# Where rotations, scale splits, signs and the last attention blocks stand in the order of a fused attention and feed-forward kernel

## The chip, the cores and the metric

The kernel runs on one core of one Trainium2 chip. The metric is device time in microseconds (us) of one execution. A core has TensorE (PE in the profile), VectorE (DVE), ScalarE (ACT), GpSimd (POOL) and SyncE (SP), which here issues most of the DMAs. [...] A number such as L590 is a line of the kernel before.

## The reference, cut to what matters

All data is float32. B = 4 sequences of S = 512 tokens, E = 1024, 16 heads of 64; the feed-forward part has 8 experts.

```python
xn = layernorm(x)
# attention, for each sequence on its own
q, k, v = (xn @ Wq), (xn @ Wk), (xn @ Wv)           # (S, 16, 64)
q, k = rotary(q), rotary(k)                          # x * cos + swap(x) * sin
logits = where(causal, q @ k.T, -1e9) / 8
s = (softmax(logits) @ v).reshape(S, E) @ Wo
# gated feed-forward with weights of -1, 0, 1
routing = softmax(xn @ gate_w.T)                     # (tokens, 8)
in_scale, out_scale = routing @ in_channel_scale, routing @ out_channel_scale
f = ((xn * in_scale) @ sign(weight).T) * out_scale + bias
out = x + s * silu(f)
```

## The kernel before

**Order of work.** PE's instructions run in the order in which the program writes them. The orders of DVE, ACT, POOL and SP are decided by a scheduler when the kernel is built, from the dependences and the program order, except for the first sequence's layernorm at the start, where DVE and ACT follow the program too, and where the program pins single instructions (`keep_in_program_order`, among them the splits of scales, L682 to L685, one half of each sign, L697, and the sums of Wo, L981). So a step that the program moves takes with it what it issues on PE exactly, and on the other engines only about.

**Projections.** `projections(b)` is a generator that yields after each matmul. For each sequence it goes through ten keys (b, g, m): g is one of four groups of four heads, m is 0 for queries, 1 for keys and 2 for values (which serve two groups at once), in the order Q, K of group 0, V of groups 0 and 1, Q, K of group 1, and the same for groups 2 and 3. Each is computed as a seven-product (Strassen-Winograd) multiplication. `project_qk` (L329) issues 28 matmuls of 128x256; DVE forms the sums of weights (`form_w`, L295) and of inputs (`form_x`, L314), and joins products into the results c[0] and c[1] (L355, L390), one per unit i of the group. `project_v` issues 56.

**Rotation.** A result c becomes a rotated query or key in `rotary` (L316): ACT swaps its 32-row blocks into sw with four copies of 32x512 (L322, L323), DVE multiplies c by the cosines (L324), POOL multiplies sw by the sines (L325) and adds both (L326). Results that are not rotated yet stand in the list `turn`. Before the change, `project_qk` rotates its first result at its own end, for queries and keys alike, and the second one in whatever projection comes next, after that one's second product.

**Slots.** The attention phase has 16 slots k = (b, g). Slot k runs the attention of group k − 1 as a list of pieces, interleaved with 84 projection matmuls (`interleave`, L859; slot 0 has 76 and no attention): after each of n pieces some 84/n matmuls follow. The usual pieces are: five transposes of the probabilities of unit w (`transpose_p`, L568); `scores_1` of the present group, with `values(w)` of the one before; five transposes of unit v; `scores_3` with `values(v)`; a wait; `scores_02`; two waits. The score pieces put matmuls on PE (L508), then DVE adds the mask (L519) and takes the maximum (L523), ACT takes exponentials (L526), DVE a reciprocal (L534), and POOL normalizes (L536). `transpose_p` puts four transposes on PE (L574) and the copy of the PSUM bank to pT on ACT for banks 0, 2 and 4 (L580) and on DVE for 1 and 3 (L578). pT has one buffer, which all units share; the PSUM ring has four banks and the scores two double banks. `values` runs 16 matmuls (L590), DVE copies the result over v (L599), and SP stores it to at_d in DRAM (L600).

**What else lies in the slots.** In slot 0 the pieces are the three steps of the router (`router`, L608) and, between them, the loading and splitting of the two channel scales:

```python
pieces = [
    routing[0],
    lambda: (load_scales(in_scale), load_scales(out_scale)),
    routing[1],
    lambda: split_scales(isc),
    routing[2],
    lambda: split_scales(osc),
```

Router step 1 is a chain of small DVE operations that ends with rex (L627 to L650); step 2 transposes rex on PE (rt, L654) and stores it. `split_scales` (L672) is three DVE operations on 128x1024 (L682, L683, L685). Scales, staged weights for the signs and the next sequence's x tiles all go through one pool of two buffers, "x". `make_sign(n)` (L690) turns a staged weight tile into -1, 0, 1 with four DVE operations of 128x512 (L697, L698, twice each). Two signs are made in each of slots 4, 8, 12 and 13, by three inserted pieces: load at the slot's start, then one sign after four pieces, another after eight. In slots with g = 1 the first two x tiles of the next sequence are loaded at the slot's start; in slots with g of 2 and 3 they are normalized and transposed.

**The seam.** After slot 15 the projections are over (L936 on): the last result is rotated, the pools of the projections are closed, and bias, the eight halves of Wo (L959) and the first stored attention rows (`load_at`, L1022) are loaded. What is left of the attention is then interleaved with the feed-forward matmuls of the first pair of row tiles (`gated(0)`, L990), in steps of four matmuls: `dense(gates, n)` runs n steps and, where n is over 1, takes one of eight subtractions on DVE that form sums of Wo after each (`sum_wo`, L981). `split` makes a high part of the scaled input on ACT (hi, L755) and a low part on DVE (lo, L756); `out_scales` puts four matmuls on PE (os, L765) into the two score banks. The order there is:

```python
for n in range(5):
    transpose_p(w, n)
split(0, 0)
values(w)
```

then two steps of `dense`, v's transposes in pairs with two steps after each, `scores_1`, `values(v)`, two steps, `scores_3`, four steps, `out_scales`, the rest of `gated(0)`, and `scores_02`. After the seam come `gated(1)` and `project_out(q)` for eight pairs of row tiles, which the change does not touch.

Of the kernel before, what the change touches and what calls it, by code (L numbers as in the profile page):

```python
# [15 lines left out]
DVE = mybir.EngineType.DVE  # L16
# [35 lines left out]
def attn_gated_ffn_kernel(  # L52
# [15 lines left out]
    nc = tc.nc  # L68
# [33 lines left out]
    osc = cp.tile([P, E], F32R, name="osc")  # L102
# [62 lines left out]
    def load_x(b, t):  # L165
        if b == 0:
            xt = X1[:, t, :]
        else:
            xt = xip.tile([P, E], F32, tag="x", name=f"x_{b}_{t}")
        nc.sync.dma_start(out=xt, in_=x[(b * TPB + t) * P : (b * TPB + t + 1) * P, :])  # L170
        xin[b, t] = xt
# [141 lines left out]
        }[n]()  # L313
        nc.vector.tensor_tensor(f, x0, x1, op=ALU.subtract)  # L314

    def rotary(u, m, c):  # L316

        sc = SCALE if m == 0 else 1.0
        rot = qk.tile([P, S], F32, tag=f"rot{m}", name="rot%d_%d_%d_%d" % (m, *u))
        sw = tmp.tile([P, S], F32, tag="sw", name="sw%d_%d_%d_%d" % (m, *u))  # L320
        for r in range(0, P, 64):
            nc.scalar.activation(sw[r : r + 32, :], c[r + 32 : r + 64, :], AF.Copy, scale=sc)  # L322
            nc.scalar.activation(sw[r + 32 : r + 64, :], c[r : r + 32, :], AF.Copy, scale=sc)  # L323
        nc.vector.scalar_tensor_tensor(rot, c, sc, cos_sb, op0=ALU.mult, op1=ALU.mult)  # L324
        nc.gpsimd.tensor_tensor(sw, sw, sin_sb, op=ALU.mult)  # L325
        nc.gpsimd.tensor_tensor(rot, rot, sw, op=ALU.add)  # L326
        (Q, K)[m][u] = rot

    def project_qk(key):  # L329

        b, g, m = key
        pos = keys.index(key)
        after = keys[pos + 1] if pos + 1 < len(keys) else None
        a11, a12, a21, a22 = quarters_w(key)
        b11, b12, b21, b22 = quarters_x(b)
        un = "%d_%d_%d" % key
        c = [tmp.tile([P, S], F32, tag="c", name=f"c_{un}_{i}") for i in range(2)]

        def product(ps, wq, xq):
            for k in range(4):  # L340
                nc.tensor.matmul(  # L341
                    ps, lhsT=wq[:, k, :], rhs=xq[:, k, :], start=(k == 0), stop=(k == 3)
                )
                yield

        def halves(n):

            ps = bank(f"pj_{un}_{n}")
            return ps, ps[:, :TH], ps[:, TH:]

        def part(n):
            return tmp.tile([P, TH], F32, tag=f"part{n}", name=f"part_{un}_{n}", bufs=1)

        def add(out, ps, x):
            nc.vector.tensor_tensor(out, ps, x, op=ALU.add)  # L355

        _, p, r = halves(1)
        yield from product(p, a11, b11)
        yield from product(r, a12, b21)
        p1 = tmp.tile([P, S], F32, tag="part1", name=f"part_{un}_1", bufs=1)[:, :TH]  # L360
        nc.scalar.copy(p1, p)
        add(c[0][:, :TH], r, p1)
        if turn:
            rotary(*turn.pop(0))
        _, p, r = halves(2)
        yield from product(r, SF[key, 3], TF[b, 3])
        if pos == 0:

            bank3 = halves(3)
            yield from product(bank3[2], SF[key, 1], TF[b, 1])  # L370
        yield from product(p, SF[key, 2], TF[b, 2])
        u2, u3 = part(2), part(3)
        add(u2, p, p1)
        add(u3, r, u2)
        if after:
            form_w(after, 3)
        if pos:
            ps, p, r = halves(3)
            yield from product(r, SF[key, 1], TF[b, 1])
        else:  # L380
            ps, p, r = bank3
        if after:
            form_w(after, 1)
            if after[2] < 2:
                form_w(after, 2)
        yield from product(p, a22, TF[b, 4])
        p5 = tmp.tile([P, S], F32, tag="part1", name=f"part_{un}_5", bufs=1)[:, :TH]
        nc.scalar.copy(p5, r)
        nc.gpsimd.tensor_tensor(u2, u2, p5, op=ALU.add)
        nc.vector.tensor_tensor(  # L390
            c[1].rearrange("p (h n) -> p h n", h=2),
            ps.rearrange("p (h n) -> p h n", h=2),
            u3[:, None, :].to_broadcast((P, 2, TH)),
            op=ALU.add,
        )
        load_w()
        _, p, _ = halves(4)
        yield from product(p, SF[key, 4], b22)
        add(c[0][:, TH:], p, u2)
        if after and after[2] < 2:  # L400
            form_w(after, 4)

        turn.extend([((b, g, i), m, c[i]) for i in range(2)])
        rotary(*turn.pop(0))

    def project_v(key):

        b, g, _ = key
# [53 lines left out]
        if turn:  # L462
            rotary(*turn.pop(0))
        yield from product(7, SF[key, 3], TF[b, 3])
        yield from product(6, SF[key, 2], TF[b, 2])
        add(u2, 6, lambda n: by_group(p1, n))
        add(u3, 7, lambda n: quarter(n, *u2))
# [24 lines left out]
    turn = []  # L492
# [375 lines left out]
    for k, (b, g) in enumerate(groups):  # L868
        pieces = []
        if k > 0:  # L870
            pieces, late = attention_pieces(k - 1, late)
        extra = []
        if g == 0:
            routing = [lambda n=n: router(b, n) for n in range(3)]
            if k == 0:
                nothing = lambda: None
                pieces = [
                    routing[0],
                    lambda: (load_scales(in_scale), load_scales(out_scale)),
                    routing[1],  # L880
                    lambda: split_scales(isc),
                    routing[2],
                    lambda: split_scales(osc),
                    nothing,
                    nothing,
                    nothing,
                ]
            else:

                if b < B - 1:  # L890
                    pieces.insert(7, routing[0])
                pieces.insert(10, routing[1])
                pieces.insert(13, routing[2])
        elif g == 1 and b + 1 < B:
            for t in range(2):
                load_x(b + 1, t)
        elif g > 1 and b + 1 < B:
            t0 = 2 * (g - 2)
            for t in range(t0, t0 + 2):
                layernorm(b + 1, t)  # L900
            extra = [
                lambda t=t, h=h: transpose_x(b + 1, t, h) for t in range(t0, t0 + 2) for h in range(2)
            ]
            if g == 2:
                extra.append(lambda: [load_x(b + 1, t) for t in (2, 3)])

        step = max(1, (len(pieces) + len(extra)) // (len(extra) + 1))
        for n, e in enumerate(extra):
            pieces.insert(min(len(pieces), (n + 1) * step + n), e)
        if len(pieces) > 18:  # L910

            pieces.append(lambda: None)
        if k in (4, 8, 12, 13):
            n = {4: 0, 8: 2, 12: 4, 13: 6}[k]
            pieces.insert(8, lambda: make_sign(n + 1))
            pieces.insert(4, lambda: make_sign(n))
            pieces.insert(0, lambda: (load_sign(n), load_sign(n + 1)))
        if b == B - 1:

            if g < 2:  # L920
                load_xn(g)
            if g in (1, 2):
                pieces.insert(3, lambda: in_scales(g - 1, score_banks))
            if g == 3:
                z_place[0] = [xip.tile([P, E], F32, tag="x", name=f"z0_{i}") for i in range(2)]
                pieces.insert(3, lambda: out_scales(0, score_banks))
        if k == 11:

            pieces.append(lambda: router(b + 1, 0))
        interleave(pieces, fill, 3 * 7 * 4 if k else 3 * 7 * 4 - 8)  # L930
        if g == NGRP - 1:
            for _ in fill:
                pass
            if b + 1 < B:
                for n in (3, 1, 2, 4):
                    form_x(b + 1, n)  # L936
                fill = projections(b + 1)
    rotary(*turn.pop(0))
    pctx.close()


# [84 lines left out]


    u0, u1 = units = [(*groups[-1], i) for i in range(2)]
    w, v = late
    sums = iter([(n, c) for n in (1, 3) for c in range(4)])  # L1030

    def dense(gates, n):
# [4 lines left out]
                if nxt:  # L1037
                    sum_wo(*nxt)

    for n in range(5):  # L1040
        transpose_p(w, n)
    split(0, 0)
    values(w)
    gates = gated(0)
    dense(gates, 2)
    split(0, 1)
    for ns in ((0, 1), (2, 3), (4,)):
        for n in ns:
            transpose_p(v, n)
        if n < 4:  # L1050
            dense(gates, 2)
    scores_1(units)
    values(v)
    dense(gates, 2)
    scores_3(units)
    dense(gates, 4)

    split(1, 0)
    out_scales(1, score_banks)
    dense(gates, 4)  # L1060
    for _ in gates:
        pass
    split(1, 1)
# [211 lines left out]
```

## Time and profile before

| what | us |
|---|---|
| three runs | 1203.40, 1203.84, 1203.88 |
| median | 1203.84 |
| profiled execution, device time | 1206.14 |
| its span | 1204.4 |
| PE busy / DVE busy / ACT busy / POOL busy | 1177.4 / 768.6 / 494.8 / 550.6 |
| mean granted clock of PE | 0.992 |

The span is the time from the first to the last instruction in the trace; the device time has 1.74 us around it. PE's busy time counts overlapping matmuls once. PEclk in the page and in the windows is the clock that PE was granted, 1.00 being full speed; [...]. A wait "PE pv L590 <- ACT pT L580" says that PE stood ahead of its instruction of line 590 on tile pv until ACT had finished the one of line 580 on tile pT. A timeline row gives the start, the duration, the engine, the line, the operation and its tiles, and in brackets the idle time ahead of it with what ended it.

### The profile page before, as it was taken

To read this page: it belongs to the slowest core of one execution; us is meant where nothing else is said; L and a number is where in the kernel's file an instruction comes from. 1 tells how busy PE (TensorE), PEld (TensorE's weight loads), DVE (VectorE), ACT (ScalarE), POOL (GpSimd) and SP (SyncE) were. 2 spreads that over 40 slices of the span, in tenths; PEclk is the share of its full clock that TensorE was granted. 3 is DMA by queue.
4 is the path that set the end of the run, shared out by engine and by line. 5 is a ranking of instruction groups with operands and counts; after the bars stand their busy time and mean duration, and the time that the engine had idled before them with its cause. 6 is when DMAs were issued, how large, how long until landed. Compare 5 with 4: busy or idle time off the path is not lost.

```text
span 1204.4 us, 16112 instructions
## 1 busy us (share of the span) xinstructions
PE 1177.4 (98%) x5864; PEld 863.1 (72%) x5864; DVE 768.6 (64%) x1380; ACT 494.8 (41%) x1121; POOL 550.6 (46%) x597
## 2 busy tenths in 40 slices
PE   9899999999999999999999999999899999999998
PEld 8788777777777777877778787777565466545664
DVE  6767767875876687487759777755656633553353
ACT  2435734543664454275545426534543121222120
POOL 0535624541653455165435615443355455544544
PEclk9899999999999999999999999999899999999999
DMA  8321423313141341314145122210503523422320
GB/s 304 110 76 68 155 79 118 111 47 114 44 158 55 107 145 48 96 62 140 53 123 202 64 84 75 79 49 19 205 10 122 181 85 127 144 83 92 110 70 35
DMA packets 60016, 121.92 MB, mean 101 GB/s; under 512 B 5025, under 2 KB 40609, under 8 KB 53921
## 3 DMA queue, kind: packets, MB, share of 16 engines
q1 hardware_dynamic: 55072, 112.11, 28.3%
q0 software_dynamic: 4576, 8.39, 2.0%
q8 instruction: 46, 0.75, 0.3%
q10 hardware_dynamic: 288, 0.39, 0.1%
q14 instruction: 34, 0.27, 0.1%
HBM read 95.45 MB, written 25.43 MB: 100 GB/s over the span
## 4 chain that ended last, share of the span: by engine, by line
PE 78%; DVE 12%; ACT 7%; issue 2%; POOL 1%; DMA 0%; ACTq 0%; DVEq 0%; POOLq 0%
PE pj L341 22%; PE wo L1112 16%; PE pj L425 13%; PE ff L990 10%; PE pv L590 5%; PE sc L508 5%; PE ptp L574 5%; DVE nmx L523 2%; ACT sw L322 2%; ACT sw L323 2%; ACT p L526 2%; DVE S L295 1%; DVE sc L519 1%; PE xtp L210 1%; PE idle L782 1%
## 5 line engine op out<-in xcount | busy, mean ns | idle before, releaser
L536 POOL TENSOR_SCALAR p<-p,rs 128x128 f32<-128x128 f32 (+3 forms) x256 | 167.0, 665 | 245.5 <-DVE rs L534 243.4
L526 ACT ACTIVATE p<-sc,nmx 128x128 f32<-128x128 f32 (+3 forms) x256 | 132.6, 524 | 175.3 <-DVE nmx L523 167.7
L341 PE MATMUL pj<-X,w 128*128 128x256 f32 x576 | 138.8, 382 | 0.2 <-ACT X L216 0.2
L325 POOL TENSOR_TENSOR sw<-sw,sin_sb 128x512 f32<-128x512 f32 x64 | 86.5, 1352 | 91.5 <-ACT sw L323 83.9
L341 PE MATMUL pj<-T,S 128*128 128x256 f32 x512 | 123.5, 383 | 0.0
L341 PEld LDWEIGHTS pj<-X,w 128*128 128x128 f32 x576 | 105.2, 190 | 14.6 <-issue 1.8
L580 ACT COPY pT<-ptp 128x512 f32<-128x512 f32 x96 | 56.0, 586 | 140.7 <-PE ptp L574 136.1
L341 PE MATMUL pj<-T,w 128*128 128x256 f32 x448 | 109.0, 385 | 0.0
L523 DVE TENSOR_REDUCE nmx<-sc 128x2 f32<-128x512 f32 (+3 forms) x128 | 103.5, 819 | 2.5
L990 PE MATMUL ff<-sg,hi 128*128 128x512 f32 x256 | 104.5, 408 | 0.0
L574 PE MATMUL ptp<-ident,p 128*128 128x128 f32 x640 | 95.3, 274 | 8.7 <-POOL p L536 4.8
L341 PEld LDWEIGHTS pj<-T,S 128*128 128x128 f32 x512 | 94.1, 191 | 12.3 <-DVE S L295 0.3
L990 PE MATMUL ff<-sg,lo 128*128 128x512 f32 x256 | 100.8, 394 | 0.0
L425 PE MATMUL pj<-w,X 128*128 128x256 f32 x416 | 99.3, 383 | 1.4 <-DVE c L390 1.4
L574 PEld LDWEIGHTS ptp<-ident,p 128*128 128x128 f32 x640 | 78.6, 141 | 27.0 <-POOL p L536 6.0
L326 POOL TENSOR_TENSOR rot<-rot,sw 128x512 f32<-128x512 f32 x64 | 94.4, 1475 | 4.9
L322 ACT ACTIVATE sw<-c 32x512 f32<-32x512 f32 x128 | 80.4, 628 | 33.7 <-DVE c L355 31.7
L341 PEld LDWEIGHTS pj<-T,w 128*128 128x128 f32 x448 | 83.8, 194 | 11.2 <-issue 0.7
L425 PEld LDWEIGHTS pj<-w,X 128*128 128x128 f32 x416 | 76.1, 190 | 13.5 <-DVE c L390 2.2
L508 PE MATMUL sc<-rot,rot 64*128 64x384 f32 (+3 forms) x512 | 82.7, 450 | 1.4 <-ACT p L526 1.4
L425 PE MATMUL pj<-w,T 128*128 128x256 f32 x352 | 83.1, 381 | 0.0
L519 DVE TENSOR_TENSOR sc<-sc,mask 128x256 f32<-128x256 f32 x128 | 53.7, 420 | 43.3 <-PE sc L508 43.1
(143 smaller groups left out, 1997.6 us busy)
## 6 DMA issues: line engine op xcount, KB each, us to landing
w<-in_wqk SPq DMA_DIRECT2D x31, 1024.0 KB, 4.8
w<-in_wv SPq DMA_DIRECT2D x16, 1024.0 KB, 5.8
x<-in_x SPq DMA_DIRECT2D x16, 512.0 KB, 3.8
xn_d<-X SPq DMA_DIRECT2D x16, 512.0 KB, 5.7
at_d<-v SPq DMA_DIRECT2D x32, 256.0 KB, 2.3
xp<-xn_d SPq DMA_DIRECT2D x16, 512.0 KB, 4.7
ap<-at_d SPq DMA_DIRECT2D x16, 512.0 KB, 4.5
xr<-in_x SPq DMA_DIRECT2D x16, 512.0 KB, 4.4
```

Of the source, the lines that this page charges most:

```text
L322: nc.scalar.activation(sw[r : r + 32, :], c[r + 32 : r + 64, :], AF.Copy, scale=sc)
L325: nc.gpsimd.tensor_tensor(sw, sw, sin_sb, op=ALU.mult)
L326: nc.gpsimd.tensor_tensor(rot, rot, sw, op=ALU.add)
L341: nc.tensor.matmul(ps, lhsT=wq[:, k, :], rhs=xq[:, k, :], start=(k == 0), stop=(k == 3))
L425: nc.tensor.matmul(ps[:, j, :], lhsT=xq[:, k, j * P : (j + 1) * P], rhs=wq[:, k, :], start=(k == 0), stop=(k == 3),)
L508: nc.tensor.matmul(ps[:, h, :], lhsT=Q[u][r : r + D, i * P : (i + 1) * P], rhs=K[u][r : r + D, : (i + 1) * P], start=True, stop=True,)
L523: nc.vector.tensor_reduce(nmx, ps, AX.X, ALU.max, negate=True)
L526: nc.scalar.activation(pt[:, h, :], ps[:, h, :], AF.Exp, bias=nmx[:, h : h + 1], accum_out=ssum[:, h : h + 1],)
L536: nc.gpsimd.tensor_scalar(pt[:, h, :], pt[:, h, :], rs[:, h : h + 1], 1.0, op0=ALU.mult, op1=ALU.mult,)
L574: nc.tensor.transpose(tp[:, k, :], probs(u, i)[:, h, j * P : (j + 1) * P], ident)
L990: nc.tensor.matmul(acc, lhsT=part[q, i][:, c, :], rhs=sg[4 * k + c // 2][:, (c % 2) * HALF : (c % 2 + 1) * HALF], start=(c == 0 and part i ...
L1112: nc.tensor.matmul(ps, lhsT=lhs[:, k, :], rhs=rhs[:, k, :], start=(k == 0), stop=(k == 3))
```

## The change

Four things are moved, and four copies go to another engine.

1. `project_qk` rotates its first result at its own end only for queries. Both rotations of keys are issued in the next projection: one after its second product as before, one later (after the sums u2 and u3 in `project_qk`, after product 7 in `project_v`).
2. In slot 0 the split of in_scale comes after the router's last step, and the split of out_scale is a piece of slot 1.
3. The four signs of slots 4 and 8 are made in slots 5 and 9. The loading of the next sequence's first two x tiles becomes a later piece of the slot with g = 1, at position 12 before the sign pieces are inserted.
4. At the seam, w's transposes and values, the last two rotations (the second one with its swap as four DVE copies) and v's first four transposes come ahead of the closing of the projections' pools, then four steps of `dense`, v's last transpose, one step, `scores_1`, `values(v)`, four steps, `scores_3`, five steps, `out_scales`, two steps and the rest.

The list of instructions is otherwise the same on every engine. As built, the four swap copies go from ACT to DVE; on SP the store of w's attention rows (at_d) comes ahead of the eight loads of Wo.

```diff
@@ -313,12 +313,16 @@
         }[n]()
         nc.vector.tensor_tensor(f, x0, x1, op=ALU.subtract)
 
-    def rotary(u, m, c):
+    def rotary(u, m, c, swap=None):
 
         sc = SCALE if m == 0 else 1.0
         rot = qk.tile([P, S], F32, tag=f"rot{m}", name="rot%d_%d_%d_%d" % (m, *u))
         sw = tmp.tile([P, S], F32, tag="sw", name="sw%d_%d_%d_%d" % (m, *u))
         for r in range(0, P, 64):
+            if swap is DVE:
+                nc.vector.tensor_copy(sw[r : r + 32, :], c[r + 32 : r + 64, :])
+                nc.vector.tensor_copy(sw[r + 32 : r + 64, :], c[r : r + 32, :])
+                continue
             nc.scalar.activation(sw[r : r + 32, :], c[r + 32 : r + 64, :], AF.Copy, scale=sc)
             nc.scalar.activation(sw[r + 32 : r + 64, :], c[r : r + 32, :], AF.Copy, scale=sc)
         nc.vector.scalar_tensor_tensor(rot, c, sc, cos_sb, op0=ALU.mult, op1=ALU.mult)
@@ -372,6 +376,8 @@
         u2, u3 = part(2), part(3)
         add(u2, p, p1)
         add(u3, r, u2)
+        if turn:
+            rotary(*turn.pop(0))
         if after:
             form_w(after, 3)
         if pos:
@@ -401,7 +407,8 @@
             form_w(after, 4)
 
         turn.extend([((b, g, i), m, c[i]) for i in range(2)])
-        rotary(*turn.pop(0))
+        if m == 0:
+            rotary(*turn.pop(0))
 
     def project_v(key):
 
@@ -462,6 +469,8 @@
         if turn:
             rotary(*turn.pop(0))
         yield from product(7, SF[key, 3], TF[b, 3])
+        if turn:
+            rotary(*turn.pop(0))
         yield from product(6, SF[key, 2], TF[b, 2])
         add(u2, 6, lambda n: by_group(p1, n))
         add(u3, 7, lambda n: quarter(n, *u2))
@@ -878,9 +887,9 @@
                     routing[0],
                     lambda: (load_scales(in_scale), load_scales(out_scale)),
                     routing[1],
+                    nothing,
+                    routing[2],
                     lambda: split_scales(isc),
-                    routing[2],
-                    lambda: split_scales(osc),
                     nothing,
                     nothing,
                     nothing,
@@ -892,8 +901,10 @@
                 pieces.insert(10, routing[1])
                 pieces.insert(13, routing[2])
         elif g == 1 and b + 1 < B:
-            for t in range(2):
-                load_x(b + 1, t)
+
+            pieces.insert(12, lambda: [load_x(b + 1, t) for t in range(2)])
+            if b == 0:
+                pieces.insert(6, lambda: split_scales(osc))
         elif g > 1 and b + 1 < B:
             t0 = 2 * (g - 2)
             for t in range(t0, t0 + 2):
@@ -910,8 +921,8 @@
         if len(pieces) > 18:
 
             pieces.append(lambda: None)
-        if k in (4, 8, 12, 13):
-            n = {4: 0, 8: 2, 12: 4, 13: 6}[k]
+        if k in (5, 9, 12, 13):
+            n = {5: 0, 9: 2, 12: 4, 13: 6}[k]
             pieces.insert(8, lambda: make_sign(n + 1))
             pieces.insert(4, lambda: make_sign(n))
             pieces.insert(0, lambda: (load_sign(n), load_sign(n + 1)))
@@ -935,7 +946,15 @@
                 for n in (3, 1, 2, 4):
                     form_x(b + 1, n)
                 fill = projections(b + 1)
-    rotary(*turn.pop(0))
+
+    w, v = late
+    for n in range(5):
+        transpose_p(w, n)
+    values(w)
+    rotary(*turn[0])
+    rotary(*turn[1], swap=DVE)
+    for n in range(4):
+        transpose_p(v, n)
     pctx.close()
 
 
@@ -1026,7 +1045,6 @@
 
 
     u0, u1 = units = [(*groups[-1], i) for i in range(2)]
-    w, v = late
     sums = iter([(n, c) for n in (1, 3) for c in range(4)])
 
     def dense(gates, n):
@@ -1037,27 +1055,21 @@
                 if nxt:
                     sum_wo(*nxt)
 
-    for n in range(5):
-        transpose_p(w, n)
     split(0, 0)
-    values(w)
     gates = gated(0)
-    dense(gates, 2)
     split(0, 1)
-    for ns in ((0, 1), (2, 3), (4,)):
-        for n in ns:
-            transpose_p(v, n)
-        if n < 4:
-            dense(gates, 2)
+    dense(gates, 4)
+    transpose_p(v, 4)
+    dense(gates, 1)
     scores_1(units)
     values(v)
-    dense(gates, 2)
+    dense(gates, 4)
     scores_3(units)
-    dense(gates, 4)
+    dense(gates, 5)
 
     split(1, 0)
     out_scales(1, score_banks)
-    dense(gates, 4)
+    dense(gates, 2)
     for _ in gates:
         pass
     split(1, 1)
```

## The prediction

> **What bounds the kernel now.** I read the page's shares first, then its 40 slices.
>
> ```profile
> PE 1177.4 (98%) x5864; PEld 863.1 (72%) x5864; DVE 768.6 (64%) x1380; ACT 494.8 (41%) x1121; POOL 550.6 (46%) x597
> ...
> PE   9899999999999999999999999999899999999998
> PEclk9899999999999999999999999999899999999999
> ```
>
> TensorE is busy 98%, so an edit pays only where PE stands or runs slowly: slices 2 and 29 (one is 30.1 us). The change leaves PE's amount of work alone: it moves when PE's operands are ready. Second view, PE's waits (us in total, times, longest):
>
> ```profile
> PE ptp L574 <- POOL p L536: 4.8, 3, 1.6
> PE pv L590 <- ACT pT L580: 3.1, 1, 3.1
> PE rt L654 <- DVE rex L650: 3.0, 1, 3.0
> PE ptp L574 <- DVE pT L578: 2.3, 4, 1.3
> PE os L765 <- ACT p L526: 1.6, 1, 1.6
> ...
> PE sc L508 <- ACT p L526: 1.4, 1, 1.4
> ```
>
> By PE's timeline they lie so: 3.04 us in slot 0 (rt, to 38.99); four gaps each in slots 4 and 8 (0.57, 0.17, 0.38, 0.70 from 215 to 246, the same from 429 to 460), 1.82 a slot; the seam's five (0.49, 1.33, 3.11, 1.40, 1.57, between 847 and 881), 7.9. The 4.8 us on POOL are the openings of slots 3, 7 and 11, which the change does not touch. Third view, windows: length, PE busy, PEld, DVE, ACT, POOL, PEclk, DMA.
>
> ```profile
> 34.70:38.10 3.40, 1.25 (x6) 0.76 (x4) 3.40 (x5) 1.88 (x3) 3.25 (x3) 1.00 0.00 0
> 38.10:44.90 6.80, 5.91 (x15) 4.79 (x16) 6.73 (x10) 0.00 (x0) 2.44 (x3) 0.50 0.31 87
> ...
> 850.50:857.30 6.80, 3.82 (x12) 1.48 (x14) 2.31 (x3) 5.50 (x10) 5.24 (x4) 0.50 1.03 419
> ...
> 881.20:884.60 3.40, 3.40 (x10) 2.74 (x9) 0.00 (x0) 1.40 (x3) 3.40 (x6) 0.50 0.03 6
> ```
>
> A long gap is paid twice: after three of them the granted clock is 0.5, and work takes double (values 4.26 us instead of 2.30). That costs 5.91/2 = 2.96 us in slot 0, and 1.9 and 1.7 at the seam. The 1.6 us gap at 154.6 drew none.
>
> [...] the windows ahead were 37 to 51% busy, the one with the 1.6 us gap 75%. [...] pT waits for eight swaps below. [...] here 0.41 us (sg, one input) against 0.68 (two).
>
> **The change part by part.** The two orders of instructions differ by four swaps that go from ACT to DVE; else they are rearranged.
>
> **Slot 0.** Start us, duration:
>
> ```profile
> 33.36 0.75 DVE L683 TENSOR_SCALAR scales<-scales,row_kind 128x1024 f32<-128x1024 f32 x1
> ...
> 35.40 2.29 DVE L685 SCALAR_TENSOR_TENSOR isc<-isc,row_kind,scales 128x1024 fp32r<-128x1024 f32 x1
> 37.61 1.23 DVE L650 COPY rex<-rhi 128x32 f32<-128x32 f32 x1
> ```
>
> The split of in_scale is woven into the router's chain: L682 (0.69), L683 (0.75) and L685 (2.29) stand ahead of rex. Now the split comes after the router's third step, so rex is done 3.7 us earlier: 38.85 − 3.7 = 35.1, 33.9 if the last copy takes 0.17 as its twin at 35.31 did. PE asks at 35.95. The gap goes (−3.04), and the half clock with it (−2.96): −6.0. The split of out_scale goes to slot 1's sixth piece, some 2.7 us of DVE (L682 0.68, L683 0.75, L685 1.28; 3.7 with a 2.29 beside POOL). Slot 1's pieces shift by it: scores_02 come ten matmuls (4.3 us) earlier, and three of POOL's rt loads (0.5 to 0.76 each) go ahead of its part of a key, which eats the 2.7 us between the last rotation (57.58) and scores_1 (60.28): 0 to 1 lost. I take −5.5, from −6 to −3 (the lower end: the half clock stays).
>
> **Slots 4 and 8.** Out of each go eight sign operations, two times (0.41 + 0.68) × 2 = 4.4 us, 5.4 with the stretched first one:
>
> ```profile
> 218.90 1.48 DVE L697 TENSOR_SCALAR sg<-wb 128x512 fp32r<-128x512 f32 x1
> ...
> 221.98 0.68 DVE L698 SCALAR_TENSOR_TENSOR sg<-wb,sg 128x512 fp32r<-128x512 f32 x1
> 222.58 0.68 DVE L578 COPY pT<-ptp 128x512 f32<-128x512 f32 x1
> ```
>
> DVE was busy 25.1 of 30 us at 210 to 240; the pT copy at 222.58, for which PE stood 0.38, comes 2.2 us earlier (1.48 + 0.68). On ACT the first pT copy gets ahead of the second key's swaps, 2.5 us, which takes the 0.57. With fewer pieces the slot's transposes begin at once; their probabilities are ready at 207.5, PE wants them at 209.0. Of 3.64 in both slots I take −3.0, from −3.6 to −1.
>
> **Slots 5 and 9** take the signs. DVE is busy 14.8 of 30 us at 270 to 300, with holes such as
>
> ```profile
> 280.04 0.43 DVE L519 TENSOR_TENSOR sc<-sc,mask 128x256 f32<-128x256 f32 x1 [3.78 <-PE sc L508]
> ```
>
> so 4.4 us cost nothing; were a sign to catch a pT copy there as in slot 4, 1.8 a slot. The loads on SP (two signs, later the next two x tiles, the third x tile after sg0 near 278) land in some 4 us and are read from 316 on: 0. Slots 12 and 13 stay.
>
> **Other key rotations.** They are issued later in program order, but the scheduler leaves the order of DVE and POOL nearly as it was; in slots 6 and 10 two pT copies move ahead of two swaps (0.63 each), and POOL's last rotation still follows at 328.9 by my count. No wait added: 0. Bounds: 0.2 us of wait is there already at 328.3 and 542, slot 2 has 0.4 us in hand; +1 in all, −0.5 where pT gains.
>
> **The seam.** ACT now:
>
> ```profile
> 852.19 0.62 ACT L323 ACTIVATE sw<-c 32x512 f32<-32x512 f32 x1
> 852.84 1.56 ACT L580 COPY pT<-ptp 128x512 f32<-128x512 f32 x3
> ```
>
> All eight swaps (5.1 us from 847.70) run before pT. In the change two pT copies lead, one follows after one swap, and the second key's swap is four DVE copies after pT3 (0.4 each [...], 0.68 as the other bound: 1.6 to 2.7 us, behind which only a rotation and lo wait). PE's list also has v's first four transposes ahead of the dense products. Walking it in order: the opening 0.49 stays; values waits 0.35 instead of 3.11 for a DVE pT copy; ff waits 0.3 for lo; the second score of scores_3 waits about 1.5 for the exponentials that free its bank; os 0.65. Sum 3.3 instead of 7.9: −4.6. Without gaps of over 1.6 no half clock: −3.6. What is late next is on SP's queue:
>
> ```profile
> 846.35 7.33 SPq L959 DMA_DIRECT2D wo<-in_wo  x8
> ...
> 858.51 0.37 SPq L600 DMA_DIRECT2D at_d<-v  x1
> ```
>
> The at_d store of w now stands ahead of the eight wo loads and waits for values, till about 853.3. The first sum of wo needs the third landing (854.04 before: issue and 1.24 us per load), now 860 to 861.5, and DVE, in order, stands before it from 858 for 2 to 3.5 us with the scores' masks behind: my 1.5 contains this, at worst 2.4. For that and a rest of half clock I take −7.5, from −10 to −4.
>
> **Sum:** −5.5 − 3.0 − 7.5 = −16.0. From the profiled execution (1206.14; span 1204.4 and 1.74 around it) that gives 1190.1; it ran 2.3 above the median of the three runs, so beside 1203.84 it is 1187.8: 1188.
>
> **The rivals.**
> (a) The wo loads behind the store eat the seam: DVE's stand, 3.5 us, goes through to scores_3 and draws a new window at half clock (1.7 to 3.4). For it: DMA share 1.0 at 850 to 860; against it: values and four steps of ff (16 matmuls, some 4 us) stand between scores_1, whose mask DVE delays, and scores_3, which needs the bank of scores_1. The seam then gives 2 to 4: about 1192.5. Chance 0.2.
> (b) Only slot 0 or only the seam gains, since the next wait stands close behind each one removed (os follows sc by 7 us): −6 to −8, 1196 to 1198. Chance 0.13.
> (c) Slower: rotations come late at scores_1 in the even slots, where the slack is 0.2 us below nothing to 2.9. Two swaps of 0.63 behind pT copies, 1.3 us, and POOL's 1.35 products queued behind them would be 2.6 a slot. In the seven even slots from 2 to 14 that is 18, over my 16: 1206. It decides from 2.3 a slot. Against it: the order on POOL is the same. Chance 0.08.
> (d) The change doesn't do what it says: split and signs land in the old places, as DVE's order is a scheduler's. The two orders speak against it; 1204, chance 0.03.
>
> **How the numbers follow.** My forecast has 0.56. Its own range, with the parts' ends not all falling together, is 1182.5 to 1193; (a) lies inside, (b) brings the upper end to 1198. 0.2% (2.4 us) is about what a measurement of this kernel can tell from no change: faster 0.88 (forecast, a, nearly all of b), same 0.04 (d, a little of c), slower 0.08.
>
> **What the changed profile would show.** Right: no rt gap at 36 to 39 and PEclk 1.00 at 38 to 45; no gaps at 215 to 246 and 429 to 460, none new at 270 to 300; no wait of pv for ACT; waits left on sc and os; DVE waiting for the wo DMA. Wrong: clock 0.5 in slices 28 to 29, a wait of sc for POOL's rot in even slots, a wait of PE for DVE in slots 5 or 9.

## The result, and the profile after

The changed kernel takes 1194.43 us (median of four runs, 1193.3 to 1196.6) against 1203.62 before (median of four on the same chip): 9.2 us less, a ratio of 0.9926 with a 95% interval of 0.9909 to 0.9943. The forecast was 1188, in a range of 1182.5 to 1198. The profiled execution took 1196.60 us with a span of 1194.9, 9.5 less than the one before. From the page of after, shares and slices:

```profile
PE 1173.2 (98%) x5864; PEld 861.5 (72%) x5864; DVE 770.1 (64%) x1384; ACT 492.5 (41%) x1117; POOL 551.3 (46%) x597
...
PE   9999999999999999999999999999999999999998
PEclk9999999999999999999999999999999999999999
```

The two dents of before (slices 2 and 29) are gone in both rows. Where PE stands is still told by its waits (us in total, times, longest):

```profile
PE ptp L583 <- POOL p L545: 6.3, 3, 2.1
PE sc L517 <- POOL rot L330: 2.9, 4, 1.1
...
PE os L774 <- ACT p L535: 1.2, 1, 1.2
PE ff L1009 <- DVE v L608: 1.1, 1, 1.1
PE sc L517 <- ACT p L535: 1.1, 1, 1.1
PE ptp L583 <- DVE pT L587: 1.0, 3, 0.7
```

The waits for rex (3.0), for ACT's pT at the seam (3.1) and for DVE's c (1.4) are gone. Two lines are worse than before: the openings of slots 3, 7 and 11 wait 6.3 us for POOL instead of 4.8, and scores wait 2.9 for POOL's rotations, a line that was not there (0.38, 1.04, 0.38, 1.05 in slots 4, 6, 8, 10). The first is paid twice in places, as windows of after show (length, PE busy, PEld, DVE, ACT, POOL, PEclk, DMA). They lie on the steps on which half clock began in this trace, at 150.67 and 580.75, 126 times 3.413 us apart:

```profile
147.25:150.66 3.41, 1.32 (x7) 0.85 (x6) 3.37 (x10) 2.64 (x9) 1.26 (x3) 1.00 0.00 0
150.66:154.08 3.42, 3.42 (x11) 2.88 (x12) 2.46 (x5) 1.28 (x5) 3.42 (x5) 0.50 0.01 2
362.27:365.69 3.42, 1.81 (x9) 1.25 (x7) 3.35 (x9) 3.23 (x10) 1.27 (x3) 1.00 0.00 0
365.69:369.10 3.41, 2.93 (x18) 2.66 (x19) 3.38 (x10) 1.28 (x5) 3.41 (x4) 1.00 0.00 0
```

Slots 3 and 7 open after the same gap of 2.08 us. In slot 3 it falls into one window of 3.41 us (PE 39% busy) and the next runs at half clock, 1.7 us lost; in slot 7 two windows share it (53% in the first), and nothing follows. Slot 11 went like slot 3 (39% from 577.33 to 580.75, half clock in the next). How the gap falls on these windows thus decides what it costs. Four profiles of other kernels below with this gap show one, one, two and three such windows, and this goes with the spread of their times.

Added up between the two profiled executions, waits and half clock by place: slot 0 −3.04 − 2.96 = −6.0; slots 4 and 8 from 3.64 to 1.09 (0.16 for pT and 0.38 for rot in the first, 0.17 and 0.38 in the second), −2.55; slots 6 and 10 +2.5 (1.04 + 1.05, and 0.22 each for x); openings 4.78 to 6.24 and two half windows, +1.5 + 3.4 = +4.9; the seam's waits 7.90 to 4.20 (0.50, 0.23, 1.14, 1.14, 1.19), −3.7, and no half clock, −3.6. The sum is −8.5 of the 9.5; the other 1.0 lies in PE's busy time and not in its waits, and is not explained.

### The profile page after: what moved, and what is told of

Same layout as the page of the kernel before. It is cut to its first block, busy times and chain, and to the rows that moved or that the text cites. A ratio compares the mean times of both kernels' runs of the same rounds, so it can differ in the third digit from the quotient of the medians.

```text
span 1194.9 us, 16113 instructions
## 1 busy us (share of the span) xinstructions
PE 1173.2 (98%) x5864; PEld 861.5 (72%) x5864; DVE 770.1 (64%) x1384; ACT 492.5 (41%) x1117; POOL 551.3 (46%) x597
## 4 chain that ended last, share of the span: by engine, by line
PE 77%; DVE 10%; ACT 6%; POOL 3%; issue 3%; DMA 1%; SPq 0%; DVEq 0%; ACTq 0%; POOLq 0%
PE pj L345 22%; PE wo L1124 16%; PE pj L432 14%; PE ff L1009 9%; PE pv L599 5%; PE ptp L583 5%; PE sc L517 4%; DVE nmx L532 3%; ACT p L535 2%; ACT sw L327 2%; ACT sw L326 2%; DVE sc L528 1%; POOL sw L329 1%; POOL p L545 1%; POOL rot L330 1%
## 5 line engine op out<-in xcount | busy, mean ns | idle before, releaser
L329 POOL TENSOR_TENSOR sw<-sw,sin_sb 128x512 f32<-128x512 f32 x64 | 91.3, 1426 | 98.7 <-ACT sw L327 90.1
L330 POOL TENSOR_TENSOR rot<-rot,sw 128x512 f32<-128x512 f32 x64 | 91.2, 1424 | 4.9
L326 ACT ACTIVATE sw<-c 32x512 f32<-32x512 f32 x126 | 79.2, 628 | 34.5 <-DVE c L359 32.5
L432 PE MATMUL pj<-w,T 128*128 128x256 f32 x352 | 85.8, 390 | 0.0
L327 ACT ACTIVATE sw<-c 32x512 f32<-32x512 f32 x126 | 79.2, 628 | 1.7
```

What stands on the lines that cost most here:

```text
L432: nc.tensor.matmul(ps[:, j, :], lhsT=xq[:, k, j * P : (j + 1) * P], rhs=wq[:, k, :], start=(k == 0), stop=(k == 3),)
```

## The experiments

Each kernel was timed against the kernel before on the same chip; a ratio is to that, with its 95% interval.

**One part at a time.** Five kernels take the kernel before and make one part of the change, or take the changed kernel and leave one part out.

Slot 0 alone:

```diff
                     routing[1],
+                    nothing,
+                    routing[2],
                     lambda: split_scales(isc),
-                    routing[2],
-                    lambda: split_scales(osc),
...
+            if b == 0:
+                pieces.insert(12, lambda: [load_x(b + 1, t) for t in range(2)])
+                pieces.insert(6, lambda: split_scales(osc))
+            else:
```

> The kernel before with only the scale splits moved (in_scale after the router, out_scale into slot 1; the next sequence's first two x tiles load later in slot 1 alone, because the buffers ask for it). Theory: slot 0 is worth 6 us by itself (3.0 of gap, 3.0 of half clock), so 1197 to 1198. Rival: the time is given back at the openings of slots 3, 7 and 11, whose wait for POOL grows from 1.6 to 2.1 once the earlier slots are quicker, and draws half clock there: 1200 or more.

Measured: 1199.59 against 1203.32, ratio 0.9965 (0.9952 to 0.9978). The rt gap is gone, the openings stay at 1.59. The gain is 3.7 by the medians (4.2 by the ratio) and not 6. Neither theory fits; the reason is in the profile of the next kernels, which still have the gap of 3.04. Windows of the seam kernel below around it:

```profile
33.55:36.96 3.41, 1.84 (x9) 1.28 (x7) 3.41 (x4) 2.44 (x5) 3.26 (x3) 1.00 0.00 0
36.96:40.37 3.41, 1.94 (x10) 1.76 (x11) 3.41 (x4) 0.00 (x0) 2.56 (x2) 1.00 0.47 154
40.37:43.79 3.42, 3.42 (x18) 3.01 (x17) 3.38 (x7) 0.37 (x1) 0.00 (x0) 1.00 0.08 19
```

Two windows share the gap, 54% and 57% busy, and the clock stays at 1.00. Six profiles of the study have this gap. Only the one of before that the prediction was made from had half clock behind it; there the window was 37% busy, and in the seam kernel, as the windows show, the emptier one was 54% busy.

Signs alone:

```diff
-            for t in range(2):
-                load_x(b + 1, t)
+            pieces.insert(12, lambda: [load_x(b + 1, t) for t in range(2)])
...
-        if k in (4, 8, 12, 13):
-            n = {4: 0, 8: 2, 12: 4, 13: 6}[k]
+        if k in (5, 9, 12, 13):
+            n = {5: 0, 9: 2, 12: 4, 13: 6}[k]
```

> The kernel before with only the signs of slots 4 and 8 made in slots 5 and 9, and the x tiles loaded later. Theory: four gaps a slot go, 3.0 to 3.6 us together, nothing is lost in slots 5 and 9: about 1200.3. Rival: without the key rotations' new order the wait of 0.57 for ACT's pT copy stays in each: about 1201.5, and slots 6 and 10 show no wait of sc for POOL's rot.

Measured: 1205.74 against 1203.32, ratio 1.0016 (1.0006 to 1.0027): slower, by little. Both expectations fell. PE's waits in this kernel have

```profile
PE ptp L574 <- DVE pT L578: 5.6, 4, 1.8
...
PE sc L508 <- POOL rot L326: 2.0, 2, 1.0
```

The second line is the wait of slots 6 and 10 (0.99 each), without any key rotation moved: it comes with the signs and the later loads of x, which this kernel moves together. The first holds one gap of 1.81 in each of slots 4 and 8 in place of the four that made 1.82. DVE's timeline shows what stands in the way there; the first two rows are of this kernel in slot 4, the fence after them has the same place of after:

```profile
211.02 2.29 DVE L314 TENSOR_TENSOR T<-X,T 128x1024 f32<-128x1024 f32 x1
213.23 0.68 DVE L578 COPY pT<-ptp 128x512 f32<-128x512 f32 x1
```

```profile
210.17 1.22 DVE L314 TENSOR_TENSOR T<-X,T 128x1024 f32<-128x1024 f32 x1
211.31 0.68 DVE L587 COPY pT<-ptp 128x512 f32<-128x512 f32 x1
211.91 1.16 DVE L328 SCALAR_TENSOR_TENSOR rot<-c,cos_sb 128x512 f32<-128x512 f32 x1
```

With the rotations as before, both (at 208.68 and 210.41) stand ahead of the pT copy, and the T form takes 2.29. In before it takes 2.29 at the same place (from 215.00 on), with 2.2 us of POOL's multiplication and addition beside it. With them issued later, the second rotation goes behind the copy, and the T form takes 1.22.

Keys alone, as in the change (the added lines stand after u3, and again after product 7 of values); at the seam there are two calls of rotary instead of one:

```diff
+        if turn:
+            rotary(*turn.pop(0))
...
-        rotary(*turn.pop(0))
+        if m == 0:
+            rotary(*turn.pop(0))
...
     rotary(*turn.pop(0))
+    rotary(*turn.pop(0))
```

> The kernel before with only the key rotations moved. Theory: alone they bring no gain and move three small things: the wait of 0.57 for ACT's pT copy goes in slots 4 and 8 (-1.1), the openings of slots 3, 7 and 11 grow from 1.6 to 2.1 (+1.4, with half clock in some executions), and the seam's ACT queue stays as full: 1203 to 1205. The waits of sc for POOL's rot in slots 6 and 10 are not there, since the later scores_02 of slots 5 and 9 cause them. Rival: they are there, 1 us each, and the time is over 1205.

Measured: 1207.44 against 1203.03, ratio 1.0031 (1.0019 to 1.0043): slower.

```profile
PE ptp L579 <- POOL p L541: 6.2, 3, 2.1
...
PE ptp L579 <- ACT pT L585: 1.1, 2, 0.6
```

The openings have grown to 2.07 and 2.08, two of the three drew half clock in its profile, and slots 4 and 8 keep their four gaps, the 0.57 for ACT too. There is no wait of sc for POOL's rot. So of the theory the openings and slots 6 and 10 were right, the 0.57 wrong, and the half clock, which I had put down as occasional, was by all signs there in most runs: six of the seven took 1207.2 to 1207.9 at mean clocks of 0.992 and 0.993, one 1204.3 at 0.994.

Seam alone (with one rotation left for it, `rotary(*turn[0], swap=DVE)`):

> The kernel before with only the seam in the new order; one key rotation is left for the seam, and its swap is made by DVE copies. Theory: the seam gains 7 us as the changed kernel's trace shows (scores_02 come 9.5 earlier, 2.4 of it from ahead of the seam): 1196 to 1197. Rival: it needs the second rotation there to hide behind: 1199.

Measured: 1201.89 against 1203.32, ratio 0.9991 (0.9983 to 0.9998), less than the rival gave. The seam's waits here are 0.48, 0.67, 1.21, 3.52, 0.82 and 1.10, 7.8 in sum: as much as before, with two windows of half clock behind them. Where the 1.4 us come from is not shown. DVE's timeline of this kernel, and of after in the fence that follows:

```profile
846.99 1.41 DVE L323 COPY sw<-c 32x512 f32<-32x512 f32 x1
848.41 1.41 DVE L324 COPY sw<-c 32x512 f32<-32x512 f32 x1
849.86 0.69 DVE L328 SCALAR_TENSOR_TENSOR rot<-c,cos_sb 128x512 f32<-128x512 f32 x1
850.46 4.03 DVE L760 TENSOR_TENSOR lo<-xp,hi 128x512 fp32r<-128x512 f32 x3
854.42 0.68 DVE L603 COPY v<-pv 128x512 f32<-128x512 f32 x1
```

```profile
848.18 0.42 DVE L323 COPY sw<-c 32x512 f32<-32x512 f32 x1
848.62 0.42 DVE L324 COPY sw<-c 32x512 f32<-32x512 f32 x1
849.07 0.69 DVE L328 SCALAR_TENSOR_TENSOR rot<-c,cos_sb 128x512 f32<-128x512 f32 x1
849.68 1.77 DVE L765 TENSOR_TENSOR lo<-xp,hi 128x512 fp32r<-128x512 f32 x1
851.37 0.68 DVE L608 COPY v<-pv 128x512 f32<-128x512 f32 x1
```

In the seam kernel the last key's first rotation, issued at the key's end, has its swap on ACT, so POOL multiplies and adds (846.72 to 849.5) just when DVE copies, and two of the copies take 1.41 instead of 0.42. Then three low parts, not one, stand ahead of the copy of v, whose bank the first feed-forward matmul needs. In the changed kernel POOL starts its rotations at 849.19, when DVE's copies are done. So the seam's new order needs the second key rotation there.

The changed kernel without the key rotations:

> The changed kernel with the key rotations issued as before (the first one at the key's own end). Theory: the waits of sc for POOL's rot (0.38, 1.04, 0.38, 1.05 in slots 4, 6, 8, 10) come from these and go, 3 to 3.8 us less than the changed kernel: 1190.5 to 1191.5; if the longer openings of slots 3, 7 and 11 come from them too, and with those the half clock, 1188. Rival: the moved rotations are what clears slots 4 and 8 (pT copies ahead of swaps on ACT), and what is won in 6 and 10 is lost there: 1193 to 1195.

Measured: 1198.44, ratio 0.9950 (0.9934 to 0.9967), 4 us more than the changed kernel by the medians (2.9 by the ratios) and more than the rival gave. It has the gaps of 1.83 and 1.82 in slots 4 and 8, waits of 0.99 and 0.98 for rot in slots 6 and 10, openings of 1.59, and a seam with 6.3 of waits and two windows of half clock. The waits of slots 6 and 10 are not the rotations'.

Keys and seam together, the rest as before:

> The kernel before with the key rotations moved and the seam in the new order, slots 0, 4, 5, 8 and 9 as before. Theory: the seam alone won 1 us because its one rotation met DVE's swap copies and lo beside POOL; with both rotations left for the seam it wins its full 7 us of the changed kernel (no half clock there), against 4 lost by the key rotations at the openings of slots 3, 7 and 11: 1199 to 1201. Rival: the seam's gain hangs on the earlier slots, and the two sums add as measured alone (+4.4 and -1.1): 1206.

Measured: 1199.82 against 1203.52, ratio 0.9969 (0.9960 to 0.9978). The theory holds: the seam's waits are 4.0 as in the changed kernel, without half clock, and the openings wait 2.09. The parts measured alone (+4.4 and −1.4 by the medians) do not add.

**What delays scores_1 in slots 6 and 10.** In the changed kernel, scores_02 of slots 5 and 9 stand three matmuls of the program later than before, since four added pieces (three for the signs, one for the loads of x) change the share of projection matmuls per piece. One empty piece more brings them forward again:

```diff
             pieces.insert(0, lambda: (load_sign(n), load_sign(n + 1)))
+            if k in (5, 9):
+                pieces.append(lambda: None)
```

> The changed kernel with one empty piece at the end of slots 5 and 9, so that scores_02 stand there after four matmuls of the product instead of eight (five before the change). Theory: the sign pieces made scores_02 of slots 5 and 9 late by 1.3 us, their softmax pushed the rotations of slots 6 and 10, and scores_1 waits 1.04 for POOL there; with the piece these waits go: 2 us less than the changed kernel, 1192 to 1192.5. Rival: the x tiles' later load or the key rotations make the wait, and it stays, 1194.4.

Measured: 1194.17 against 1203.03, ratio 0.9922 (0.9902 to 0.9942). The waits for rot in slots 6 and 10 fell from 1.04 and 1.05 to 0.32 and 0.63, and those for x are gone, 1.6 us of waits. The runs stand at 1192.3 and 1192.5 (mean clock 0.999) and at 1195.9 and 1196.2 (0.996), so half clock hides the gain in the median: that the place of scores_02 makes most of the wait is shown, its price in time is not.

**What makes the openings wait.** Slot 3 begins with a transpose of probabilities that slot 2's last exponentials and POOL must have finished. ACT's timeline of after, shortly before:

```profile
140.86 1.28 ACT L188 ACT_TABLE_LOAD   x1
142.15 0.29 ACT L188 ACTIVATE std<-mv,eps 128x1 f32<-128x1 f32 x1
142.47 1.28 ACT L535 ACT_TABLE_LOAD   x1
...
145.01 1.28 ACT L188 ACT_TABLE_LOAD   x1
146.36 0.30 ACT L188 ACTIVATE std<-mv,eps 128x1 f32<-128x1 f32 x1
146.67 1.28 ACT L535 ACT_TABLE_LOAD   x1
```

Two square roots of one column each bring four table loads, 5.1 us, and I took them for the cause. The edit puts both roots together:

```diff
             for t in range(t0, t0 + 2):
-                layernorm(b + 1, t)
+                half_statistics(b + 1, t, 0)
+                half_statistics(b + 1, t, 1)
+            for t in range(t0, t0 + 2):
+                deviation(b + 1, t)
+            for t in range(t0, t0 + 2):
+                normalize(b + 1, t)
```

> The changed kernel with the layernorm statistics of a slot's two x tiles ahead of both square roots, so that ACT switches its table once for both instead of twice. Theory: the openings of slots 3, 7 and 11 (2.08 us each) wait for exponentials behind two pairs of table loads of 1.28 us; one pair less and they open without a wait, and no half clock follows: 6.2 us less than the changed kernel at its profile, 1188 to 1190. Rival: DVE's statistics and normalization beside POOL set that chain, and the wait stays over 1 us: 1192 to 1194.

Measured: 1188.11 against 1203.03, ratio 0.9870 (0.9856 to 0.9885). In its waits the line for POOL's p has gone and these have come:

```profile
PE xtp L210 <- DVE x L196: 3.1, 3, 1.4
...
PE ptp L583 <- DVE v L458: 1.2, 3, 0.4
```

The openings wait 0.40 for DVE; there is no half clock ahead of the span's end, and the four runs lie within 0.6 us. The new cost is 1.40 in slots 6 and 10 for the first x tile, whose normalization now comes behind both tiles' statistics on DVE.

That the edit takes the wait away is shown; that the table loads made it is not. The edit does two things: ahead of each opening one pair of loads falls away, and the second tile's statistics go ahead of the first tile's normalization on DVE. They were not tried apart, and the trace of after speaks for the second. DVE, between the first root and the opening of slot 3 at 150.53:

```profile
142.68 1.87 DVE L196 TENSOR_SCALAR x<-x,mv,rstd 128x1024 f32<-128x1024 f32 x1
...
144.81 1.27 DVE L180 BATCH_NORM_STATS2 bn<-x 128x6 f32<-128x512 f32 x2
146.11 0.21 DVE L186 BATCH_NORM_AGGREGATE mv<-bn 128x2 f32<-128x12 f32 x1
...
146.71 1.29 DVE L532 TENSOR_REDUCE nmx<-sc 128x2 f32<-128x256 f32 x2
147.92 0.75 DVE L458 TENSOR_TENSOR v<-pj,part 128x256 f32<-128x256 f32 x2
...
148.77 0.81 DVE L196 TENSOR_SCALAR x<-x,mv,rstd 128x1024 f32<-128x1024 f32 x1
149.50 0.16 DVE L543 RECIPROCAL rs<-ssum 128x2 f32<-128x2 f32 x1
```

From the first normalization on, DVE has no idle time over 0.15 us up to the last of these rows, and the reciprocal for which POOL stood 2.15 us comes last. The second pair of loads (145.01 and 146.67) lies beside these rows, and the second root, at 146.36, starts when its aggregate is done. The chain of releases that the profile follows back from the opening runs through DVE as well, in after and in before; of the loads it has only the one ahead of the first root, which the edit leaves. So the rival named the right chain, though its time was wrong.

The same edit in the kernel before, for the second pair of x tiles alone (slots with g of 3):

> The kernel before with the square roots of the second pair of x tiles put together (slots with g of 3 alone), nothing else. Theory: the openings' wait of 1.6 us for POOL is the table loads' there too, and goes to 0.4 or less: 3.6 us or more less than before, 1199 to 1199.5; no half clock was drawn there. Rival: the openings only became costly with the key rotations, and before gains under 2 us: 1201.5.

Measured: 1198.88 against 1203.52, ratio 0.9960 (0.9947 to 0.9973). The openings fall from 1.6 to 0.40 there as well. What the key rotations added to them is seen in DVE's first normalization, which stands in that chain, beside POOL's last key rotation. In slot 2 it takes 1.86 to 1.88 in the five kernels that have the key rotations moved and the roots apart, after among them, and 1.40 in the five that have both as before. The difference of 0.47 is the growth of the openings (1.60 to 2.08 in slot 3).

**The store ahead of the Wo loads.** SP in after, and then DVE:

```profile
852.08 0.36 SPq L609 DMA_DIRECT2D at_d<-v  x1
852.49 4.05 SPq L978 DMA_DIRECT2D wo<-in_wo  x8
```

```profile
856.60 0.68 DVE L1019 TENSOR_TENSOR z<-ff,z 128x512 f32<-128x512 f32 x1
859.54 1.29 DVE L1000 TENSOR_TENSOR xp<-wo,wo 128x512 f32<-128x512 f32 x2 [2.26 <-DMA wo<-in_wo]
```

```diff
-        nc.sync.dma_start(
+        queue = nc.scalar if u == (B - 1, NGRP - 2, 0) else nc.sync
+        queue.dma_start(
```

> The changed kernel with the at_d store of w at the seam issued from ACT's queue, so that SP issues the eight loads of Wo without waiting for values. Theory: DVE's stand of 2.26 us for the third load goes, the scores' masks come 2 us earlier, and the waits of sc (1.14) and os (1.19) for ACT shrink by 1 to 2 us together: 1193. Rival: those two waits are set by the softmax chain after the scores, not by the stand, and the time stays within 0.5 us.

Measured: 1194.72 against 1203.03, ratio 0.9921 (0.9906 to 0.9936). The loads are issued from 840.71 on, DVE no longer stands, and the wait of sc for ACT at the seam (1.14) is gone; the wait of os stays, 1.10. So the first of the two waits hung on the stand, and the second did not. In time nothing can be told from the changed kernel, again with half clock between (1192.3 at a clock of 0.998, 1194.7 to 1194.9 at 0.996).

**Put together.** Roots together (slots with g of 3 alone), the empty piece, and the store on ACT's queue:

> The changed kernel with three edits together: square roots together (slots with g of 3 alone), one empty piece in slots 5 and 9, the at_d store of w from ACT's queue. Theory: the parts add, since each takes another wait: openings 2.08 to 0.4 (-5 and no half clock), sc in slots 6 and 10 1.04 to 0.3 or 0.6 without the xtp wait of 1.40 that putting together all roots brought, sc at the seam 1.14 to 0: 1185.5 to 1187. Rival: the softmax chains move together and some of the waits come back elsewhere: 1188 or more.

Measured: 1185.71 against 1203.52, ratio 0.9853 (0.9836 to 0.9869): faster than both kernels, by 17.8 and by some 9 us. The largest of its waits, beside the start:

```profile
PE sc L517 <- POOL rot L330: 1.7, 4, 0.6
...
PE ptp L583 <- DVE v L458: 1.2, 3, 0.4
PE ff L1021 <- DVE v L608: 1.1, 1, 1.1
PE os L775 <- ACT p L535: 1.1, 1, 1.1
```

The waits add as expected, each in its own place, and the mean clock of all four runs is 1.000. One more edit, on the ff line, keeps DVE's copy of v ahead of the first low part by program order:

> The combined kernel with DVE's copy of w's values put ahead of the first low part at the seam. Theory: the first feed-forward matmul waits 1.13 for that copy, since its bank is the one the values were in; with the copy first it starts 1.1 earlier, but its second matmul then needs the low part, which comes two pT copies later: 0 to 0.6 less than the combined kernel. Rival: the wait only changes its name, and the time is the same within 0.2.

Measured: 1186.42 against 1203.52, ratio 0.9860 (0.9845 to 0.9874), no better than the combined kernel. The wait of ff is 1.55 instead of 1.14, now for lo: it changed its name, as the rival said, and got longer. The profiled execution also has a window of half clock at the seam, behind the wait of os (clock 0.999).

## Why the prediction was right or wrong

It had the direction and the range; the forecast of 1188 was 6.4 us too low. Between the two profiled executions its three terms came to −15.9 (−6.0, −2.55, −7.3) where −16.0 were forecast. What it lacked are two costs that it put at nothing: +2.5 in slots 6 and 10, and +4.9 at the openings. The forecast's own range ended at 1193. That 1194.43 lies in the range stated is owed to rival (b), for which its end was put at 1198, and (b) did not happen: that part is luck. Step by step:

- **Slot 0 (−5.5):** the gap went as worked out (−3.04). The half clock's 2.96 was mis-sized: of six profiles with that gap one shows it, and slot 0 alone gained 3.7. The sum was taken off the median in full, though the 2.3 us by which the profiled execution stood above the median were a sign that most runs have nothing of this 2.96. The 52 runs of before beside the experiments stand in groups: 46 at 1201.8 to 1204.1 with mean clocks of 0.993 to 0.997, and six near 1206.1 at 0.992 to 0.993, where the profiled one lies. (A small slip without weight: rex, with the short last copy, would by the prediction's own figures be done at 34.1 and not 33.9.)
- **Slots 4 and 8 (−3.0):** 2.55 of waits went. The prediction gave them to fewer DVE operations and to ACT's pT copy getting ahead of the second key's swaps, and did not say that each needs the other: the signs' leaving alone leaves 1.81 a slot, the key rotations alone leave all four gaps, the 0.57 for ACT too, and both together clear nearly all.
- **Slots 5 and 9, "cost nothing":** right for the DVE holes, wrong for the slots. The step that failed: the added pieces were costed by their instructions alone. That they move scores_02 by three matmuls was not carried into slots 6 and 10, where the prediction itself had found no slack (0.2 us of wait at 328.3 and 542). The price is 2.5 of waits, of which the empty piece took back 1.6.
- **"The openings of slots 3, 7 and 11, which the change does not touch", and "other key rotations: 0":** wrong. The later rotations add 0.47 to each through DVE beside POOL, and 2.08 drew half clock where 1.6 had not: +1.5 and, in the profile, two windows of 1.7. The prediction read 75% for PE's share in the window with the gap of 1.6, far from the 37 to 51% ahead of half clock. But its windows, 152.0 to 155.4 and 155.4 to 158.8, cut the gap in two. The starts of half clock in before (38.12, 850.49, 881.21) lie 238 and 9 times 3.413 us apart, and on the windows that they fix the gap lies in one:

```profile
154.18:157.59 3.41, 1.81 (x11) 1.33 (x10) 3.19 (x10) 1.86 (x8) 2.13 (x4) 1.00 0.00 0
```

That is 53%, hardly more than the 51% ahead of the half clock at 881.21. Nor did that half clock need a gap of over 1.6: the one ahead of it, os, was 1.57. The roots together took 6.3 off the changed kernel, the largest gain of the single edits, though 1.2 of each opening's wait was there before the change as well.

- **The seam (−7.5):** −3.7 of waits and −3.6 of half clock. Inside it, DVE stood 2.26 for Wo where 2 to 3.5 were forecast, sc waited 1.14 (1.5), os 1.19 (0.65), and ff 1.14 (0.3), the last for the bank under the copy of v and not for lo.
- **The rivals:** (a) was seen in the trace, DVE's stand and a wait of sc behind it, at a size that the forecast held. (c) named a real wait, sc for POOL's rot in even slots, but with the wrong culprit; it came to 1.04 and not 2.6. (b) did not happen: slot 0, slots 4 and 8 and the seam all gained. Neither did (d): splits and signs went to their new places.

That signs or keys alone are slower than before, and the seam alone hardly faster, I had not foreseen: by their ratios the parts measured alone make −4.2 + 1.9 + 3.7 − 1.1 = +0.3 us, the whole −8.9. The parts need each other at the seam and in slots 4 and 8, as the runs with two of them together show.

## What to carry to other kernels

A profiled execution above the median may hold an event that most runs don't have; look for it before its cost is put into a sum. Where pieces share a slot by count, adding an empty or a cheap piece changes the place of the others, so follow the expensive ones into the next slot. Waits in places that an edit does not touch still belong to the sum when they can grow to a length that half clock followed, here 1.6 us that became 2.1 (half clock behind two of the three in after, behind none in before). And an edit that takes a wait away does not yet say what made it, when the edit changes the order on two engines: follow the chain back through the trace first.

## What the runs showed of the hardware

- Half clock began only on a fixed grid in the traces of before and after: within each its starts lie whole multiples of 3.413 us apart (in before 238 of them, 812.37 us, between the first two and 9, 30.72 us, between the next; in after 126, 430.08 us), and ahead of the span's end it lasted one step or two (3.413 or 6.827 us). Outside the seam it began behind windows of this grid with PE 37% busy in slot 0 of before and 39% at the openings of slots 3 and 11 of after, and not behind windows of 53 and 54% at the openings of slots 3 and 11 of before, 53% at that of slot 7 of after, and 54 and 57% in slot 0 of the seam kernel. Of the 15 openings with a gap of about 2.08 in five profiles it followed nine. At the seam of before it began behind windows of 43 and 51% and not behind one of 59%. So partly idle windows were enough; whether PE's busy share in such a window decides alone is not shown.
- At half clock the 128x256 matmuls of after (152.2 to 153.5) followed each other every 0.427 us instead of 0.216 (146.1 to 147.4). It is this distance that doubles: the recorded duration of one went from 0.379 to 0.634 only.
- A DVE copy of 32x512 took 0.42 us alone (after, 848.18) and 1.41 beside POOL's multiplication or addition (the seam kernel, 846.99 and 848.41). The normalization of 128x1024 took 0.81 alone (after, 148.77), 1.40 with 0.85 us of POOL's addition beside it (before, 148.86) and 1.87 with 1.27 us of it (after, 142.68).
- Switching ACT between square root and exponential cost 1.28 us each way, four times the 0.29 us of the root itself, and the next instruction began right behind it (in after, 142.15 after a load from 140.86).
